# A fused attention and expert layer on one core: r by Strassen's scheme, and a reciprocal made of an exponential

## The chip, the cores and the metric

The kernel runs on one core of one Trainium2 chip. TensorE (PE) multiplies matrices, VectorE (DVE) works elementwise, ScalarE (ACT) evaluates functions, GpSimd (POOL) sets up constants and issues gathers and scatters, SyncE (SP) issues most other DMAs. Each works through its own queue in order, and they wait for one another at semaphores. The metric is the time of the whole program in device microseconds; a lower time is better.

## The reference

x is one sequence of 2048 tokens of 512 channels. xn is the layer norm of x. The result is x plus two parts.

The first is an RWKV attention: r, v, k = xn W, and, channel by channel along the tokens,

```
no = max(o, u + k);  A = exp(o - no);  Bc = exp(u + k - no)
y  = (A p + Bc v) / (A q + Bc)
o, p, q are carried on, with the decay w = -exp(time_decay)
out1 = (sigmoid(r) * y) W_out
```

The second is a mixture of experts. A softmax over 12 experts picks two per token; eight of them are small networks (silu(g) * u, 256 wide), four pass xn through, and the two chosen outputs are added with their weights.

## The kernel before, in words

**Tiling.** Channels lie on the 128 partitions in four column groups c = 0..3, tokens in four blocks b = 0..3 of 512. A unit (b, c) is one 128 x 512 piece of the recurrence. The 16 units go in the order (0,0), (1,0), (0,1), (1,1) ..., (1,3), (2,0), (3,0) ..., (3,3). The tokens of the experts are gathered into 25 tiles of 128.

**Products.** k and v of a pair of blocks are made by Strassen's scheme in Winograd's form: seven products p1 to p7 in place of eight per column group, each of two matmul steps (`two`), on sums of weights (`sum_weights`) and sums of blocks (`sum_x`). Their partial sums are taken out of PSUM in the middle, by copies on ACT (p1, p2) and additions on DVE (p3 to p7). r is made plainly: `r(b, c, h)` does two of four matmul steps, and after the fourth ACT takes exp(-r) out of PSUM into the tile that `kvr_tile` names. A matmul step in float32 shows as two instructions in the profile.

**The recurrence.** `scan(b, c)` is a generator in five stages. (1) DVE: a scan for the running maximum (L477), then a2 and b2 (L479, L480). (2) ACT: Exp of both (L482, L483). (3) DVE: the scans of the two sums (L490, L492), with b2 v between (L491). (4) DVE: den = b2 cf + sq (L497), den = (er + 1) den (L498), num = bv cf + sp (L500). (5) ACT copies the state on (L503, L504), DVE takes the reciprocal of den (L505) and multiplies num with it into yT (L506). So sigmoid(r) is part of the one division.

**Experts.** Tile i: a gather by POOL (xg), a reshaping copy on ACT (xp, L775), a transposing DMA (xq), a copy on ACT (xgT, L783), eight matmul instructions (pg, L795), tanh on ACT (th, L803), two operations on DVE (th L804, act L806), a copy on ACT (ap, L820), a transposing DMA (aq), a copy on ACT (actT, L827), four matmul instructions (po, L836), a scaled copy on ACT (yo, L840) and a scatter that adds into the output (POOL). `first_half(i)` holds pg and act of tile i, the ap of tile i-1 and the actT of tile i-2, `second_half(i)` the xgT of tile i+1, the xp of tile i+2 and the po of tile i-2.

**Order.** The schedule is manual: every engine executes in the order in which the Python code emits. From the experts on, a table sets that order. `plan(at, what)` enters one piece at a time in the table's own units; the pieces are sorted by it and emitted. Products and the output rows of blocks 0 and 1 (`attention_row`) lie one behind the other, the stages of unit u at (u-1) * unit + 4, 8, 10, 13 and 16, the halves of tile i at spread * i and spread * (i + 0.6). `unit` and `spread` follow from the number of product steps left (`left`). Behind the table come block 2's output rows, with the last stages of unit (3,3) between them, and then block 3's.

**Buffers.** PSUM pools of two banks each: ps_mm (px and r), ps_tr (py, pz), ps_gu (pg and transposes), ps_o (po and pw). The `base` pool holds the rows of xn that `attention_row` needs (three buffers); SP's queue loads them.

Of the kernel before, what the change touches and what calls it, by code (L numbers as in the profile page):

```python
# [35 lines left out]
P = 128  # L36
# [11 lines left out]
SCALE = 1.5  # L48
EPS = 1e-5
LOW = -3.0e38  # L50
O_INIT = -1.0e38
TILES = 25
MAX_TILES = 40
# [6 lines left out]
def layer(ctx: ExitStack, tc: tile.TileContext, x, w_rvk, w_out, decay, first, cls, ebias, gu, down, out):  # L60
    nc = tc.nc

    def pool(name, bufs, **kw):
        return ctx.enter_context(tc.tile_pool(name=name, bufs=bufs, **kw))
# [5 lines left out]
    gathered = pool("gathered", 2)  # L70
    wk1 = pool("wk1", 1)
    rows = pool("rows", 3)
    basep = pool("base", 3)
    rp = pool("route", 1)
    small = pool("small", 2)
    kvrp = pool("kvr", 1)
# [64 lines left out]
    make_identity(nc, ident)  # L141
    eps_sb = const.tile([P, 2], F32, tag="eps", name="eps_sb")
    nc.gpsimd.memset(eps_sb[:, 0:1], EPS)

    quarters = const.tile([P, ET], F32, tag="quarters", name="quarters")
    nc.gpsimd.tensor_add(quarters, ident[:, 0:ET], ident[:, QW : QW + ET])
# [130 lines left out]
    def kvr_tile(name, b, c):  # L277

        last = slots[name]
        n = last.index(min(last))  # L280
        last[n] = units.index((b, c))
        kvr[b, c, name] = kvrp.tile([P, TB], F32, tag=f"{name}{n}", name=f"{name}{b}_{c}")
        return kvr[b, c, name]
# [56 lines left out]
    def p1(b, c):  # L340
        ps = bank(ps_mm, "mm", f"px{b}_{c}")
        yield from two(ps, a11, xnT[b][:, 0:2], c, True)
        nc.scalar.copy(kvr_tile("v", b, c), ps)
        yield

    def p2(b, c):
        ps = banks[f"px{b}_{c}"]
        yield from two(ps, a12, xnT[b][:, 2:4], c, False)
        nc.scalar.copy(kvr_tile("k", b, c), ps)
        ready.add(("k", b, c))  # L350
        yield
# [3 lines left out]
    def p6(b, c):  # L355
        ps = bank(ps_tr, "tr", f"py{b}_{c}")
        yield from two(ps, s2, ts[b, 0][:, 1], c, True)
        out_ = kvr_tile("k", b + 1, c)
        if (b, c) < (0, 2):
            deferred.append((out_, kvr[b, c, "v"], ps))  # L360
        else:
            nc.vector.tensor_add(out_, kvr[b, c, "v"], ps)
        yield

    def p7(b, c):
        ps = banks[f"py{b}_{c}"]
        yield from two(ps, s3, ts[b, 1][:, 0], c, False)
        nc.vector.tensor_add(kvr_tile("v", b + 1, c), kvr[b, c, "v"], ps)
        yield
# [11 lines left out]
    def p4(b, c):  # L381
        ps = banks[f"py{b}_{c}"]
        yield from two(ps, a22, ts[b, 1][:, 1], c, False)
        v = kvr[b, c, "v"]
        nc.vector.tensor_add(v, v, ps)
        ready.add(("v", b, c))
        yield
# [11 lines left out]
    def r(b, c, h):  # L399

        if h == 0:
            if (b, c) == (0, 0):
                bank(ps_gu, "gu", f"pr{b}_{c}")
            else:
                bank(ps_mm, "mm", f"pr{b}_{c}")
        ps = banks[f"pr{b}_{c}"]
        for k in (2 * h, 2 * h + 1):
            nc.tensor.matmul(  # L408
                ps, wrvk_sb[0][:, k, c * P : (c + 1) * P], xnT[b][:, k, :], start=(k == 0), stop=(k == CC - 1)
            )  # L410
            if k == CC - 1:
                nc.scalar.activation(kvr_tile("r", b, c), ps, AF.Exp, scale=-1.0)
            yield

    def all_products():

        rest = iter([r(b, 3, h) for b in (0, 1) for h in (0, 1)])
        for part, c in ((p1, 0), (p1, 1), (p2, 0), (p2, 1), (p1, 2), (p1, 3), (r, 0), (p2, 2), (r, 1), (p2, 3)):
            yield from r(0, 0, c) if part is r else part(0, c)
        for c in range(3):  # L420
            for b in (0, 1):
                if (b, c) == (1, 2):
                    yield from p6(0, 0)
                    yield from p6(0, 1)
                if (b, c) != (0, 0):
                    yield from r(b, c, 0)
                    yield from r(b, c, 1)
        for part, c in (
            (p7, 0), (p7, 1), (p4, 0), (p5, 0), (p4, 1), (p3, 0),
            (p5, 1), (p6, 2), (r, 0), (p3, 1), (p6, 3), (r, 0), (p7, 2), (p7, 3),  # L430
            (p4, 2), (p4, 3), (r, 1), (p5, 2), (r, 1), (p5, 3), (p3, 2),
        ):
            yield from next(rest) if part is r else part(0, c)
        yield from p1(2, 0)
        yield from r(2, 0, 0)
        yield from p3(0, 3)
        for c in range(CC):
            if c:
                yield from p1(2, c)
                yield from r(2, c, 0)  # L440
            yield from p6(2, c)
            yield from r(2, c, 1)
            yield from p2(2, c)
            yield from p7(2, c)
            yield from r(3, c, 0)
            yield from p5(2, c)
            yield from p4(2, c)
            yield from r(3, c, 1)
            yield from p3(2, c)

    products = all_products()

# [7 lines left out]
    def scan(b, c):  # L460

        n = f"{b}_{c}"
        s = state[c]
        w, cf = wdec[:, c : c + 1], cfac[:, c : c + 1]
        assert ("k", b, c) in ready
        k = kvr[b, c, "k"]
        if c == 0:

            yT[b] = place.tile([P, NJ, CC, P], F32, tag=("s8", "s9", "s2", "s3")[b], name=f"yT{b}")


        obv = wk1.tile([P, 3, TB + 1], F32, tag="obv", name=f"obv{n}")
        nc.vector.tensor_copy(obv[:, :, 0:1], s[:, 0:3].unsqueeze(2))
        o, bs, bvs = (obv[:, m, 0:TB] for m in range(3))
        o2, b2, bv = (obv[:, m, 1 : TB + 1] for m in range(3))

        nc.vector.tensor_tensor_scan(o2, w.to_broadcast([P, TB]), k, s[:, 0:1], ALU.add, ALU.max)  # L477
        a2 = wk.tile([P, TB], F32, tag="a2", name=f"a2{n}")
        nc.vector.scalar_tensor_tensor(a2, o, w, o2, ALU.add, ALU.subtract)  # L479
        nc.vector.tensor_sub(b2, k, o2)  # L480
        yield
        nc.scalar.activation(a2, a2, AF.Exp)  # L482
        nc.scalar.activation(b2, b2, AF.Exp)  # L483
        yield

        assert ("v", b, c) in ready
        v = kvr[b, c, "v"]
        sums = wk1.tile([P, 2, TB], F32, tag="sums", name=f"sums{n}")
        sq, sp = sums[:, 0, :], sums[:, 1, :]
        nc.vector.tensor_tensor_scan(sq, bs, a2, s[:, 3:4], ALU.add, ALU.mult)  # L490
        nc.vector.tensor_mul(bv, b2, v)  # L491
        nc.vector.tensor_tensor_scan(sp, bvs, a2, s[:, 4:5], ALU.add, ALU.mult)  # L492
        yield

        er = kvr[b, c, "r"]
        den = wk1.tile([P, TB], F32, tag="den", name=f"den{n}")
        nc.vector.scalar_tensor_tensor(den, b2, cf, sq, ALU.mult, ALU.add)  # L497
        nc.vector.scalar_tensor_tensor(den, er, 1.0, den, ALU.add, ALU.mult)  # L498
        num = wk.tile([P, TB], F32, tag="a2", name=f"num{n}")
        nc.vector.scalar_tensor_tensor(num, bv, cf, sp, ALU.mult, ALU.add)  # L500
        yield
        if b + 1 < NTB:
            nc.scalar.copy(s[:, 0:3].unsqueeze(2), obv[:, :, TB : TB + 1])  # L503
            nc.scalar.copy(s[:, 3:5].unsqueeze(2), sums[:, :, TB - 1 : TB])  # L504
        nc.vector.reciprocal(den, den)  # L505
        nc.vector.tensor_mul(  # L506
            yT[b][:, :, c, :], num.rearrange("p (j t) -> p j t", j=NJ), den.rearrange("p (j t) -> p j t", j=NJ)
        )
        yield

# [449 lines left out]

    ONE = 0.86
    ROWS = [(b, j) for b in (0, 1) for j in range(NJ)]
    left = [products] * (16 * 11 - done[0])
    late = []

    def add_row(n):
# [2 lines left out]
    def attention_row(b, j):  # L969
        i = b * NJ + j  # L970
        po = ps_o.tile([P, C], F32, tag="o", name=f"pw{i}")
        for c in range(CC):
            nc.tensor.matmul(  # L973
                po, yT[b][:, j, c, :], wout_sb[:, c, :], start=(c == 0), stop=(c == CC - 1)
            )
            if c < CC - 1:
                yield
        xn = xrows[i]
        if b == 1:

            xrows[i] = yT[b][:, j].rearrange("p c t -> p (c t)")
            late.append(i)
        nc.vector.scalar_tensor_tensor(xrows[i], xn, zw[:, i : i + 1], po, ALU.mult, ALU.add)
        if b == 0 and j % 2:
            add_row(i - 1)
            add_row(i)
        yield
# [6 lines left out]
        table.append((at, iter([(what, *args)]) if args else what))  # L994

    plan(0.5, stages[0])
    plan(3, stages[0])
    for u in range(1, len(units)):

        for at in (4, 8, 10, 13, 16)[: 2 if u == len(units) - 1 else 5]:  # L1000
            plan((u - 1) * unit + at, stages[u])

    begin = 7 * unit + 1
# [18 lines left out]
    for _, work in sorted(table, key=lambda entry: entry[0]):  # L1022
        todo = next(work, None)
        if todo:
            todo[0](*todo[1:])
    for j, stops in enumerate((1, 2, 0, 0)):
        whole(attention(NTB - 2, [j]))
        for _ in range(stops):
            next(stages[-1])
# [73 lines left out]
```

## Time and profile before

| | |
|---|---|
| median of 3 runs | 379.38 us (378.77 to 379.68) |
| the profiled execution's own time | 379.29 us |
| its span | 377.5 us |
| PE busy | 358.2 us (95%) |
| DVE busy | 308.9 us (82%) |
| ACT busy | 161.5 us (43%) |
| reciprocals (L505), 16 | 53.5 us, 3345 ns each |
| matmuls of r (L408), 128 | 60.6 us busy |
| granted clock of PE | 1.0 |

The span is the profiled execution from first to last instruction; the rest of its time lies around it. A line of the groups gives line, engine, operation, output and inputs with shapes, count, then busy time in all and the mean of one in ns, then the idle time of the engine before it and what ended it. A line of the waits reads: engine, tile and line that waited, what it waited for, microseconds in all, times, the longest. In the timeline a line is start, duration, engine, line, operation, and in brackets the idle time before it with what ended it. Matmuls overlap, so a mean of 593 ns per instruction stands for one every 0.43 us.

### The profile page before, as it was taken

How to read it: one execution, taken by the hardware profiler on the slowest of the kernel's cores; microseconds unless marked ns; L12 is line 12 of the kernel's file. 1: busy time of each engine (PE TensorE's matmuls, PEld its weight loads, DVE VectorE, ACT ScalarE, POOL GpSimd, SP SyncE). 2: the span in 40 equal slices, each digit the busy share in tenths (PEclk: the TensorE clock that was granted, in tenths of full speed). 3: DMA queues.
4: the chain of work that ended last, by engine and by line, in shares of the span. 5: the costliest groups of instructions: out<-in, count | busy, mean ns of one | idle time of the engine just before them, and what ended most of it. 6: DMA issues, size and time to landing. Idle time of an engine off the chain costs nothing.

```text
span 377.5 us, 3504 instructions
## 1 busy us (share of the span) xinstructions
PE 358.2 (95%) x970; PEld 164.9 (44%) x970; DVE 308.9 (82%) x450; ACT 161.5 (43%) x274; POOL 91.4 (24%) x118
## 2 busy tenths in 40 slices
PE   0899998999999999999999999999999999999995
PEld 0565444543444444444444444444444444444343
DVE  4879899989997997987987779597769786959951
ACT  1677311232653554554556453636354555423000
POOL 5000300210203233322232224133144321102450
PEclk9999999999999999999999999999999999999999
DMA  7998944643657898889898998999999999767497
GB/s 268 399 356 322 334 141 162 227 91 132 177 126 220 257 264 250 251 230 260 220 262 237 272 265 222 271 233 319 258 280 277 290 264 248 195 188 166 93 191 191
DMA packets 63029, 88.80 MB, mean 235 GB/s; under 512 B 42208, under 2 KB 42592, under 8 KB 59232
## 3 DMA queue, kind: packets, MB, share of 16 engines
q1 hardware_dynamic: 55472, 67.85, 61.5%
q0 software_dynamic: 7536, 20.71, 23.5%
q8 instruction: 8, 0.13, 0.1%
q14 instruction: 13, 0.11, 0.1%
HBM read 63.78 MB, written 19.40 MB: 220 GB/s over the span
## 4 chain that ended last, share of the span: by engine, by line
PE 73%; DVE 17%; DMA 5%; ACT 2%; issue 2%; SPq 0%; DVEq 0%
PE pg L795 22%; PE po L836 10%; PE pr L408 9%; PE py L325 9%; PE pw L973 7%; PE pz L325 6%; PE px L325 4%; PE pw L921 4%; DMA x<-in_x_dram 3%; DVE den L505 3%; DMA wrvk<-in_w_rvk_dram 2%; DVE tok L687 2%; DVE sums L490 1%; DVE obv L477 1%; DVE st L212 1%
## 5 line engine op out<-in xcount | busy, mean ns | idle before, releaser
L795 PE MATMUL pg<-gw,xgT 128*128 128x512 f32 x200 | 90.2, 593 | 1.5 <-ACT xgT L783 1.5
L841 POOL DMA_INDIRECT out_dram<-yo,to_i x25 | 45.7, 1826 | 165.0 <-ACT yo L840 114.5
L408 PE MATMUL pr<-xnT,wrvk 128*128 128x512 f32 x128 | 60.6, 593 | 0.0
L795 PEld LDWEIGHTS pg<-gw,xgT 128*128 128x128 f32 x200 | 37.8, 190 | 49.3 <-issue 45.7
L505 DVE RECIPROCAL den<-den 128x512 f32<-128x512 f32 x16 | 53.5, 3345 | 0.0
L836 PE MATMUL po<-dw,actT 128*128 128x512 f32 x100 | 46.9, 593 | 0.5 <-ACT actT L814 0.5
L803 ACT ACTIVATE th<-pg 128x256 f32<-128x256 f32 x25 | 9.6, 384 | 85.0 <-PE pg L795 85.0
L733 POOL DMA_INDIRECT xg<-xs,token_i x25 | 27.0, 1080 | 61.9 <-ACT xp L775 28.3
L408 PEld LDWEIGHTS pr<-xnT,wrvk 128*128 128x128 f32 x128 | 24.1, 190 | 29.2 <-issue 29.2
L804 DVE SCALAR_TENSOR_TENSOR th<-th,pg 128x256 f32<-128x256 f32 x25 | 10.5, 419 | 32.1 <-ACT th L803 32.0
L325 PE MATMUL px<-xnT,wrvk 128*128 128x512 f32 x64 | 32.3, 604 | 0.0
L325 PE MATMUL py<-t,wrvk 128*128 128x512 f32 x64 | 30.7, 594 | 0.0
L783 ACT COPY xgT<-xq 128x1024 uint16<-128x1024 uint16 x25 | 28.9, 1156 | 3.9 <-DMA xq<-xp 3.8
L921 PE MATMUL pw<-wout_sb,yT 128*128 128x512 f32 (+1 forms) x72 | 28.2, 548 | 2.0 <-DVE xrows L934 1.5
L973 PE MATMUL pw<-wout_sb,yT 128*128 128x512 f32 x64 | 30.1, 592 | 0.0
L836 PEld LDWEIGHTS po<-dw,actT 128*128 128x128 f32 x100 | 18.9, 190 | 24.2 <-issue 22.7
L775 ACT COPY xp<-xg 128x1024 uint16<-128x1024 uint16 x25 | 26.1, 1044 | 5.6 <-DMA xq<-xp 4.5
L840 ACT ACTIVATE yo<-po,wplace 128x512 f32<-128x512 f32 x25 | 17.2, 686 | 23.2 <-PE po L836 23.0
L490 DVE TENSOR_TENSOR_SCAN sums<-obv,state,a 128x512 f32<-128x512 f32 x16 | 20.5, 1282 | 4.1 <-ACT obv L483 4.0
L492 DVE TENSOR_TENSOR_SCAN sums<-obv,state,a 128x512 f32<-128x512 f32 x16 | 20.5, 1284 | 0.6
L921 PEld LDWEIGHTS pw<-wout_sb,yT 128*128 128x128 f32 x72 | 13.5, 190 | 17.0 <-issue 13.4
L477 DVE TENSOR_TENSOR_SCAN obv<-wdec,state,k 128x512 f32<-128x512 f32 x16 | 20.5, 1280 | 0.0
(171 smaller groups left out, 459.0 us busy)
## 6 DMA issues: line engine op xcount, KB each, us to landing
gw<-in_gu_dram SPq DMA_DIRECT2D x25, 1024.0 KB, 5.5
dw<-in_down_dram SPq DMA_DIRECT2D x25, 512.0 KB, 5.9
x<-in_x_dram SPq DMA_DIRECT2D x16, 256.0 KB, 5.3
xs<-x SPq DMA_DIRECT2D x16, 256.0 KB, 4.9
wrvk<-in_w_rvk_dram SPq DMA_DIRECT2D x3, 1024.0 KB, 7.2
xrow<-xs SPq DMA_DIRECT2D x8, 256.0 KB, 7.0
xrows<-xs SPq DMA_DIRECT2D x8, 256.0 KB, 5.2
wout_sb<-in_w_out_dram SPq DMA_DIRECT2D x1, 1024.0 KB, 10.6
```

The costliest lines, as they stand in the source:

```text
L325: nc.tensor.matmul(ps, a[:, k, c * P : (c + 1) * P], x[:, k], start=(start and k == 0), stop=(k == 1), skip_group_check=True,)
L408: nc.tensor.matmul(ps, wrvk_sb[0][:, k, c * P : (c + 1) * P], xnT[b][:, k, :], start=(k == 0), stop=(k == CC - 1))
L477: nc.vector.tensor_tensor_scan(o2, w.to_broadcast([P, TB]), k, s[:, 0:1], ALU.add, ALU.max)
L505: nc.vector.reciprocal(den, den)
L733: nc.gpsimd.indirect_dma_start(out=xg, out_offset=None, in_=xs, in_offset=bass.IndirectOffsetOnAxis(ap=token[:, i : i + 1], axis=0),)
L775: nc.scalar.copy(xp, st[i]["xg"].bitcast(U16).rearrange("p (c h) -> p h c", h=2))
L783: nc.scalar.copy(xgT.bitcast(U16).rearrange("p c (t h) -> p c t h", h=2), st[i]["xq"].rearrange("p (h c) t -> p c t h", h=2),)
L795: nc.tensor.matmul(pg, st[i]["xgT"][:, c, :], st[i]["w"][:, c, :], start=(c == 0), stop=(c == CC - 1))
L836: nc.tensor.matmul(po, st[i]["actT"][:, c, :], st[i]["d"][:, c, :], start=(c == 0), stop=(c == IC - 1))
L841: nc.gpsimd.indirect_dma_start(out=out, out_offset=bass.IndirectOffsetOnAxis(ap=to[:, i : i + 1], axis=0), in_=yo, in_offset=None, compute ...
L921: nc.tensor.matmul(po[:, hs], yT[b][:, j, c, :], wout_sb[:, c, hs], start=(c == 0), stop=(c == CC - 1),)
L973: nc.tensor.matmul(po, yT[b][:, j, c, :], wout_sb[:, c, :], start=(c == 0), stop=(c == CC - 1))
```

## The change

Four things change in the text.

- r is taken out as tanh(r/2) instead of exp(-r), by the same one ACT operation. sigmoid(r) is then (tanh(r/2) + 1) / 2: num is multiplied by (tanh + 1), and the half goes into the reciprocal's factors.
- r of blocks 2 and 3 is made by Strassen's scheme too. Here the two halves of the weights are two neighbouring column groups, so there are seven products q1 to q7 for c = 0, 1 and seven for c = 2, 3. Sums of weights are made in place by `sum_weights_r` (four DVE operations of 128 x 256), the block sums are those that v and k use. q1 is copied out by ACT, q2 by a Tanh on ACT, the other five by DVE additions, and three finished tiles get their Tanh in place (`r_done`). A new order of p and q products stands in `all_products`.
- The reciprocal of den becomes: z = exp(-ln2/2^23 * bits(den) + seed) on ACT, with den's bits read as an integer; f = -2 den z on DVE (in den's place); (f + 1)^2 by Square on ACT; (f + 2) z, its product with num, and the product with ((f + 1)^2 + 1) on DVE. z and the square lie in the buffer of the two sums. The scan has six stages instead of five, planned at 4, 8, 10, 13, 14.5 and 16.5.
- The `base` pool has two buffers instead of three, and block 0's output rows are written in place into yT, as block 1's were.

The diff, cut to its core:

```diff
-    basep = pool("base", 3)
+    basep = pool("base", 2)
...
+    seed = const.tile([P, 2], F32, tag="seed", name="seed")
+    nc.gpsimd.memset(seed[:, 0:1], LN2 * (127.0 - 0.043 - 1.0))
+    nc.gpsimd.memset(seed[:, 1:2], 1.0)
...
-                nc.scalar.activation(kvr_tile("r", b, c), ps, AF.Exp, scale=-1.0)
+                nc.scalar.activation(kvr_tile("r", b, c), ps, AF.Tanh, scale=0.5)
...
+    def sum_weights_r(c):
+        one, two_ = slice(c * P, (c + 1) * P), slice((c + 1) * P, (c + 2) * P)
+        s1_ = sr[:, :, c // 2 * P : (c // 2 + 1) * P]
+        nc.vector.tensor_add(s1_, wr[:, 0:2, two_], wr[:, 2:4, two_])
+        nc.vector.tensor_sub(wr[:, 0:2, two_], wr[:, 0:2, one], wr[:, 0:2, two_])
+        nc.vector.tensor_sub(wr[:, 0:2, one], s1_, wr[:, 0:2, one])
+        nc.vector.tensor_sub(wr[:, 2:4, one], wr[:, 2:4, one], wr[:, 0:2, one])
+
+    def r_done(b, c):
+        t = kvr[b, c, "r"]
+        nc.scalar.activation(t, t, AF.Tanh, scale=0.5)
...
+    def q(n, b, c):
...
+        yield from two(ps, a, z, col, first_)
+        if n == 1:
+            nc.scalar.copy(kvr_tile("r", b, c + 1), ps)
+        elif n == 2:
+            nc.scalar.activation(kvr_tile("r", b, c), ps, AF.Tanh, scale=0.5)
+            sum_weights_r(c)
+        elif n == 6:
+            nc.vector.tensor_add(kvr_tile("r", b + 1, c), kvr[b, c + 1, "r"], ps)
+        elif n == 7:
+            nc.vector.tensor_add(kvr_tile("r", b + 1, c + 1), kvr[b, c + 1, "r"], ps)
+        else:
+            d, e = {4: (b, c + 1), 5: (b + 1, c + 1), 3: (b + 1, c)}[n]
+            nc.vector.tensor_add(t, t, ps)
+            r_done(d, e)
...
+            order_ = (
+                (p6, q, 2, p2, p7, q, 6, p5, p4, q, 7, p3),
+                (p1, q, 4, p6, p2, q, 5, p7, q, 3, p5, q, -1, p4, q, -2, p3),
+                (p1, q, 6, p6, p2, p7, q, 7, p5, p4, q, 5, p3, q, 3),
+                (p1, p6, p2, p7, p4, q, -4, p5, p3),
+            )[c]
...
-        nc.vector.scalar_tensor_tensor(den, er, 1.0, den, ALU.add, ALU.mult)
         num = wk.tile([P, TB], F32, tag="a2", name=f"num{n}")
         nc.vector.scalar_tensor_tensor(num, bv, cf, sp, ALU.mult, ALU.add)
+        nc.vector.scalar_tensor_tensor(num, kvr[b, c, "r"], 1.0, num, ALU.add, ALU.mult)
         yield
...
-        nc.vector.reciprocal(den, den)
-        nc.vector.tensor_mul(
-            yT[b][:, :, c, :], num.rearrange("p (j t) -> p j t", j=NJ), den.rearrange("p (j t) -> p j t", j=NJ)
+        z, sqr = sq, sp
+        nc.scalar.activation(z, den.bitcast(I32), AF.Exp, bias=seed[:, 0:1], scale=-LN2 / 2**23)
+        nc.vector.scalar_tensor_tensor(den, den, -2.0, z, ALU.mult, ALU.mult)
+        yield
+        nc.scalar.activation(sqr, den, AF.Square, bias=seed[:, 1:2])
+        nc.vector.scalar_tensor_tensor(den, den, 2.0, z, ALU.add, ALU.mult)
+        nc.vector.tensor_mul(num, num, den)
+        nc.vector.scalar_tensor_tensor(
+            yT[b][:, :, c, :], sqr.rearrange(j4, j=NJ), 1.0, num.rearrange(j4, j=NJ), ALU.add, ALU.mult
         )
...
-    left = [products] * (16 * 11 - done[0])
+    left = [products] * (16 * 11 - 4 - done[0])
...
-    plan(3, stages[0])
+    plan(2, stages[0])
+    plan(3.5, stages[0])
...
-        for at in (4, 8, 10, 13, 16)[: 2 if u == len(units) - 1 else 5]:
+        for at in (4, 8, 10, 13, 14.5, 16.5)[: 2 if u == len(units) - 1 else 6]:
...
-    for j, stops in enumerate((1, 2, 0, 0)):
+    for j, stops in enumerate((1, 3, 0, 0)):
```

## The prediction

> **What bounds the kernel now.** I read the page first (busy shares, the chain that ended last), then the waits of TensorE (PE), the busy time by stage, and last the timeline of one expert tile.
>
> ```profile
> PE 358.2 (95%) x970; PEld 164.9 (44%) x970; DVE 308.9 (82%) x450; ACT 161.5 (43%) x274; POOL 91.4 (24%) x118
> PE 73%; DVE 17%; DMA 5%; ACT 2%; issue 2%; SPq 0%; DVEq 0%
> ```
> The chain is mostly PE.
>
> ```profile
> PE pg L795 <- ACT xgT L783: 1.5, 1, 1.5
> PE pw L921 <- DVE xrows L934: 1.5, 1, 1.5
> ```
> The waits of PE: from 66 us on, hardly any. The first is at 95 us, where ScalarE (ACT) made xgT1 late because an Exp ahead of it in its queue waited for VectorE (DVE). The second is in the tail.
>
> ```profile
> 95.00:215.00 120.00, 119.85 (x279) 53.02 (x280) 103.97 (x127) 62.26 (x107) 32.26 (x22) 1.00 0.87 231
> 215.00:332.00 117.00, 117.00 (x275) 51.87 (x275) 92.86 (x116) 57.67 (x93) 35.52 (x25) 1.00 1.03 263
> 332.00:378.00 46.00, 39.61 (x100) 18.27 (x98) 31.11 (x37) 5.79 (x12) 11.89 (x11) 1.00 0.71 158
> ```
> Busy time by stage (PE, weight loads, DVE, ACT, POOL, clock, DMA): from 95 to 332 us PE has no gap at all. A microsecond of matmul less there is a microsecond less, and a new wait of PE there is a microsecond more. In the tail DVE's chain decides.
>
> The timeline of one tile (number 6; its pg begins at S = 145.47), first DVE, then ACT:
>
> ```profile
> 149.35 0.42 DVE L804 SCALAR_TENSOR_TENSOR th<-th,pg 128x256 f32<-128x256 f32 x1 [2.27 <-ACT th L803]
> 149.81 0.42 DVE L806 TENSOR_TENSOR act<-th,pg 128x256 f32<-128x256 f32 x1
> 150.15 1.28 DVE L490 TENSOR_TENSOR_SCAN sums<-obv,state,a 128x512 f32<-128x512 f32 x1
> 151.34 0.67 DVE L491 TENSOR_TENSOR obv<-obv,v 128x512 f32<-128x512 f32 x1
> 152.04 1.28 DVE L492 TENSOR_TENSOR_SCAN sums<-obv,state,a 128x512 f32<-128x512 f32 x1
> 153.25 0.73 DVE L497 SCALAR_TENSOR_TENSOR den<-obv,cfac,sums 128x512 f32<-128x512 f32 x1
> 155.28 3.35 DVE L505 RECIPROCAL den<-den 128x512 f32<-128x512 f32 x1
> ```
> ```profile
> 148.94 0.38 ACT L803 ACTIVATE th<-pg 128x256 f32<-128x256 f32 x1 [0.74 <-PE pg L795]
> 151.14 1.17 ACT L783 COPY xgT<-xq 128x1024 uint16<-128x1024 uint16 x1
> ```
> Every tile PE's pg releases ACT's th at S+3.47, and that releases DVE's th at S+3.88. All that stands behind th in DVE's queue is later: here den ends at S+8.5. ACT makes the next tile's xgT at S+5.7 to 6.8, long before PE needs it (S+10.3), because nothing ahead of it in ACT's queue waits for that late part of DVE.
>
> **The change, part by part.** Prices:
>
> ```profile
> L505 DVE RECIPROCAL den<-den 128x512 f32<-128x512 f32 x16 | 53.5, 3345 | 0.0
> L506 DVE TENSOR_TENSOR yT<-num,den 128x512 f32<-128x512 f32 x16 | 11.1, 692 | 0.5
> L840 ACT ACTIVATE yo<-po,wplace 128x512 f32<-128x512 f32 x25 | 17.2, 686 | 23.2 <-PE po L836 23.0
> ```
>
> PE. The r products of blocks 2 and 3 go from 32 to 28 (7 of 8 per pair of column groups). One product is two matmuls of 0.429 us (8 of pg take 3.43): 4 x 0.858 = 3.43 us less.
>
> DVE. Per unit, 3.35 + 0.69 (yT) + 0.70 (er) go and five operations of 0.70 come: -1.24, 16 times -19.8 us. To the r products come ten additions out of PSUM (0.68 each, 6.8) and eight of 128x256 for the weight sums, which the trace lacks. Bounds are the 256-element copy (0.29) and the 512-element add (0.69); I take 0.42, the row with the same count (L806), together 3.4. DVE loses 9.6 us, but it does not bound the middle.
>
> ACT. Per unit an Exp and a Square come, both with a column as bias. Bounds 0.60 (L412, no column) and 0.81 (L234, two); one column is L840's 0.69, which I take: +22 us, and two copies more. ACT would be half busy; its load is not the matter, its order is. [...]
>
> POOL and SP. Two memsets go before the first work. The base pool falls from three buffers to two: each of the eight xrow loads in SP's queue now waits for the addition two rows back (218.3, 233.2, 251.1 ...: some 15 us apart). It is issued about when the row before it is added, so that wait has passed 15 us earlier: nothing, and without that cover a wait in SP's queue would hold gw and the transposes behind it. POOL's row additions still wait for the same DVE instruction.
>
> The unit's chain is now DVE den, ACT Exp, DVE, ACT Square, DVE three times. Three things follow.
>
> Start: in unit (0,0), den at 83.92 leads by the steps below to a yT that ends at 89.6 instead of 90.04, and a k addition (0.6) that stood behind yT goes into the gap at Square. The next scan starts 1.0 earlier, and so xgT1: PE's idle 1.54 shrinks to 0.5. Gain 1.0.
>
> Tail: for each of the last two units the chain from den to yT was 0.78+0.61+0.66+3.38+0.69 = 6.1; it is now den 0.67, num 0.77, num 0.61, 0.72, Square with two hand-overs 0.80, 0.73, 0.73, 0.69 = 5.7. In the first of them an addition of v comes in ahead of den (+0.6) and one of k leaves the queue behind yT for the gap at Square (-0.6). Gain 2 x 0.42 = 0.85.
>
> Middle: ACT's queue now holds Exp, Square or a tanh of r that wait for DVE, and in this program's order some stand ahead of an xgT, th or actT that PE needs. I walked the built queues from tile to tile with the steps of the timeline (start to start: th 0.46, act 0.34, scan 1.2, mul 0.70, add 0.60, dependent operation 0.76, hand-over 0.05, ACT's next start 0.10 before the end). S is the start of each tile's own pg, tiles are 10.3 apart. PE stops at:
>
> 1. Tile 2 (pg2): pg1 94.05; DVE's first refining step is behind th1 and act1, ends 100.8; Square 101.55, tanh r 102.0, xgT2 103.1. PE is there at 94.05+3.54+5x0.858 = 101.9: 1.25.
> 2. Tile 5 (po3): between act4 and den of unit (1,1) stand sum_x's four operations (4.7), the sums (3.1) and two additions (1.2), so den ends 14.4 after tile 4's start, at S+4.05; Exp, a copy, Square (behind num, num, step: 6.8), ap4, th5, actT3 8.17. PE at S+6.0: 2.2.
> 3. Tile 6 (pg7): behind th6 and act6 stand the sums and the four weight additions; den ends S+10.15, Exp 10.9, xgT7 11.95. PE at 3.43+7x0.858 = 9.44: 2.55.
> 4. Tile 9 (pg10): the addition of r(2,1) ends S+8.0; its tanh, two Exps, xgT10 10.8. PE at 10.3: 0.5.
> 5. Tile 15 (pg16): sums, k addition, den 9.1, Exp 9.84, xgT16 10.9. PE at 9.44: 1.5.
> 6. Tile 19 (q3 and pg20): r(3,3)'s addition ends 8.7, its tanh, Square, xgT20 11.0. PE at 10.3: 0.75.
> 7. Tile 20 (po18): r(3,2)'s addition ends S+5.0; its tanh, ap19, th20, actT18 7.05. PE at 6.0: 0.95.
> 8. Tile 22 (p4 of column 3): it directly follows p7, in whose bank it goes on, so it waits for v(3,3)'s addition, which stands behind num and ends S+11.7. PE at 9.44: 2.3.
>
> Sum 12.0. At the other tiles the same walk leaves margins, the smallest 0.5 (pg9). Bounds: at the lower prices (0.60 on ACT, 0.29 for a weight addition) 0.1 goes at each and 0.5 more at the third, together some 1.2; at the upper (0.81, 0.69) some 2 come. What the walk leaves out bounds it from below: nothing at all, if each of these instructions finds its wait over.
>
> The sum goes against the profiled execution, 379.29 (span 377.5 and 1.79 around it; the median of the three runs is 379.38): 379.29 - 3.43 - 1.0 - 0.85 + 12.0 = 386.0.
>
> [...]
>
> **Rivals.**
> - The stalls hardly occur (faster). For it: PE's 3.43 is certain, DVE is freed of 9.6, PE waited only once for ACT before. Against it: an in-order ACT wait is just what that one wait was. With no stall 374.0; it decides below 5.3 us of stalls. Forecast for it 374 to 378.5.
> - Half of the stalls, because my walk puts DVE too late at th: 6 us, 380.0. Against it: th at S+3.88 is a measured step, and DVE waits for it in 15 of 25 tiles.
> - More than my eight: DMA is at 1.03 of its engines from 215 us, and ACT's xgT already waited twice for a transpose (3.8 us). Late xp and ap copies then cost tiles more: 390 to 394.
> [...]
>
> **How the numbers follow.** About 0.2% (0.8 us) is what a measurement can tell here from no change. Likeliest, stalls of 9 to 15: 0.60, own range 383 to 389. Half the stalls (378.6 to 383): 0.16, of which 0.05 within 0.2%. Few (374 to 378.5): 0.17. More (above 389): 0.07. The range 376.5 to 389.5 leaves out the 0.06 above it and 0.08 at the fast end.
>
> **What would show it.** PE's waits should name ACT xgT at about four places and ACT actT at two, 2 to 2.6 us the longest, and DVE v once for py near the end; ACT's waits for DVE should grow by an Exp, a Square and r. Matmuls of r should take 3.4 us less and the middle be longer all the same. DVE's busy time should fall by some 10 us, with new idle time in front of the second refining step. I am wrong if PE's waits from 95 us to the last pg sum to under 5 us.

## The result, and the profile after

The changed kernel takes 393.17 us (median of four executions, 390.28 to 396.92) where the kernel before takes 379.07. The ratio is 1.0347, 95% interval 1.0266 to 1.0428 (the comparison leaves disturbed executions out). It is slower, by about 13 us; I had forecast 386.0 with a range up to 389.5. The direction and the places were right, the size was not.

The profiled execution took 390.28, with a span of 388.5. First its page: the engines' busy times, then the slices of PE and DVE.

```profile
span 388.5 us, 3554 instructions
...
PE 360.0 (93%) x962; PEld 163.3 (42%) x962; DVE 297.6 (77%) x500; ACT 183.8 (47%) x308; POOL 91.3 (23%) x120
...
PE   0999998999899979799999999899999997998995
...
DVE  5779999899886896786878787768677767568861
```

PE has eight matmuls fewer (962 against 970), DVE has 11.3 us less to do and ACT 22.3 more. And yet the span is 11.0 longer: PE, which was at 9 in every slice of the middle, now has holes. The view of waits says for whom. Its columns: the waiting instruction, the one waited for, us in total, times, the longest.

```profile
PE pg L862 <- ACT xgT L850: 6.7, 6, 2.8
PE po L903 <- ACT actT L894: 2.9, 2, 2.2
PE py L329 <- DVE v L372: 2.3, 1, 2.3
PE po L903 <- ACT actT L881: 1.5, 1, 1.5
```

Neither xgT nor actT has anything to do with the change. ACT's own waits show why they are late: three of the instructions that the change put into ACT's queue wait for DVE there, and what is queued behind them waits too.

```profile
ACT sums L566 <- DVE den L555: 23.3, 12, 5.5
...
ACT r L435 <- DVE r L468: 14.5, 5, 3.6
ACT sums L569 <- DVE den L567: 9.8, 8, 2.0
```

These 47.6 us are mostly idle time that cost nothing; what costs is where one of them holds up an xgT or an actT that TensorE is already waiting for. The timeline at tile 6 (start, duration, engine, line, operation; in brackets the idle time before it and who ended it):

```profile
153.15 1.28 DVE L550 TENSOR_TENSOR_SCAN sums<-obv,state,a 128x512 f32<-128x512 f32 x1
...
154.14 1.88 PE L329 MATMUL py<-t,wrvk 128*128 128x512 f32 x4
...
155.78 0.42 DVE L431 TENSOR_TENSOR wrvk<-wrvk 128x256 f32<-128x256 f32 x1
156.12 0.75 DVE L555 SCALAR_TENSOR_TENSOR den<-obv,cfac,sums 128x512 f32<-128x512 f32 x1
...
156.96 0.72 ACT L566 ACTIVATE sums<-den,seed 128x512 f32<-128x512 int32 x1 [2.29 <-DVE den L555]
...
157.59 1.15 ACT L850 COPY xgT<-xq 128x1024 uint16<-128x1024 uint16 x1
...
158.79 1.55 PE L862 MATMUL pg<-gw,xgT 128*128 128x512 f32 x3 [2.77 <-ACT xgT L850]
```

DVE does the four additions of r weights (L428 to L431, 154.35 to 156.1), then den; ACT's Exp (L566) waits 2.29 us for den; xgT stands behind the Exp; PE has had nothing to do for 2.77 us when pg7 starts. From start to start (154.14 to 158.79, less four matmuls of 0.429) the stop costs 2.93, and the eight matmuls behind it take 0.11 more than 3.43.

The second thing that the profile shows I had not forecast. Behind the stop at p4 of column 3 eight matmuls of pg23 take 5.21 us instead of 3.60, and nothing waits for anything:

```profile
327.67 1.25 PE L329 MATMUL py<-t,wrvk 128*128 128x512 f32 x2 [2.28 <-DVE v L372]
...
328.72 5.21 PE L862 MATMUL pg<-gw,xgT 128*128 128x512 f32 x8
...
333.76 1.02 PE L329 MATMUL py<-t,wrvk 128*128 128x512 f32 x2
```

The windows around it tell why. After the busy times of the engines the row ends with the granted clock, the DMA share and GB/s: 1.00 before, 0.72 over six us, 1.00 again.

```profile
318.00:328.00 10.00, 7.72 (x19) 3.27 (x18) 8.05 (x12) 6.49 (x10) 1.99 (x2) 1.00 0.91 254
328.00:334.00 6.00, 6.00 (x11) 2.49 (x10) 0.22 (x1) 0.04 (x1) 0.00 (x0) 0.72 0.64 163
334.00:340.00 6.00, 6.00 (x15) 2.66 (x14) 5.18 (x9) 3.27 (x5) 0.60 (x1) 1.00 0.25 58
```

The drop costs 1.6 us in these eight matmuls. The mean clock of the execution is 0.996. Of the other three one has 0.996 too and takes 391.52; those with 0.991 and 0.987 take 394.83 and 396.92.

### The profile page after: what moved, and what is told of

Read it like the earlier page. It is cut to its first block, busy times and chain, and to the rows that moved or that the text cites. A ratio compares the mean times of both kernels' runs of the same rounds, so it can differ in the third digit from the quotient of the medians.

```text
span 388.5 us, 3554 instructions
## 1 busy us (share of the span) xinstructions
PE 360.0 (93%) x962; PEld 163.3 (42%) x962; DVE 297.6 (77%) x500; ACT 183.8 (47%) x308; POOL 91.3 (23%) x120
## 5 line engine op out<-in xcount | busy, mean ns | idle before, releaser
L862 PE MATMUL pg<-gw,xgT 128*128 128x512 f32 x200 | 92.5, 605 | 6.7 <-ACT xgT L850 6.7
L412 PE MATMUL pr<-xnT,wrvk 128*128 128x512 f32 x64 | 29.4, 594 | 0.0
L570 DVE SCALAR_TENSOR_TENSOR den<-den,sums 128x512 f32<-128x512 f32 x16 | 11.1, 692 | 16.8 <-ACT sums L569 16.0
L566 ACT ACTIVATE sums<-den,seed 128x512 f32<-128x512 int32 x16 | 11.6, 722 | 23.4 <-DVE den L555 23.3
```

The lines of the kernel that those rows point to most:

```text
L412: nc.tensor.matmul(ps, wrvk_sb[0][:, k, c * P : (c + 1) * P], xnT[b][:, k, :], start=(k == 0), stop=(k == CC - 1))
L862: nc.tensor.matmul(pg, st[i]["xgT"][:, c, :], st[i]["w"][:, c, :], start=(c == 0), stop=(c == CC - 1))
```

## The experiments

Theory A is that of the prediction: waits for DVE, put into ACT's in-order queue ahead of xgT, actT or th (and a wait of PE for DVE at p4), stop PE; to it I now add that the clock can fall behind such a stop (0.72 over 328 to 334 us above). Rival B: ACT and DVE simply have too much to do, and the stops only show where. Rivals C1 and C2: one of the two parts alone does it, the reciprocal or Strassen's r. Each kernel is compared with runs of the kernel before on the same chip; all times are medians, and all kernels do the whole computation.

**The changed kernel again (after_again).** No edit.

> The changed kernel once more, as the base for the others. Both theories: its time lies again between 390 and 397. If the TensorE clock gate has a part in it, the mean granted clock (0.996, 0.991, 0.987 in earlier executions) should account for the differences between executions: 0.001 of clock on a span of 390 is 0.4 us.

Measured: 393.21 (392.86 to 398.57), ratio 1.0387 (1.0275 to 1.0499). By their mean clock the eight executions of this kernel are: 390.3 and 391.5 at 0.996; 393.3 and 394.8 at 0.991; 392.9, 393.1 and 396.9 at 0.987; 398.6 at 0.983. The steps of the clock are those of whole drops: 3.41 us at half the clock, as from 328.54 to 331.96 us in the first profile, cost 1.7 of 390, or 0.004 of the mean clock. But the clock does not account for all differences, as I had expected it to: three executions at 0.987 differ by 4 us, and two of them are shorter than both at 0.991. Something else varies too (the kernel before, at 0.998 to 1.000, takes 378.3 to 383.1 on one chip), and the record does not show what. The profiled execution (0.987) has the same waits to 0.1 us and three drops, behind the stops of 2.23, 2.76 and 2.28 us; they cost 1.6 to 1.7 each. Its windows:

```profile
141.00:148.00 7.00, 6.15 (x11) 2.65 (x12) 6.21 (x11) 5.72 (x9) 2.21 (x2) 0.76 0.57 152
160.00:166.00 6.00, 5.69 (x10) 2.54 (x11) 3.06 (x5) 3.22 (x7) 3.06 (x2) 0.72 0.60 104
330.00:337.00 7.00, 6.49 (x11) 2.79 (x12) 1.05 (x2) 0.20 (x1) 0.00 (x0) 0.76 0.70 170
```

So the first profiled execution was a lucky one: the same stops, one drop instead of three. The last section has what the traces show of that.

**The new reciprocal alone (recip_only).**

```diff
-        yield from q(1, 2, 0)
+        yield from r(2, 0, 0)
...
-            for part in order_:
...
+            yield from p6(2, c)
+            yield from r(2, c, 1)
+            yield from p2(2, c)
+            yield from p7(2, c)
+            yield from r(3, c, 0)
+            yield from p5(2, c)
+            yield from p4(2, c)
+            yield from r(3, c, 1)
+            yield from p3(2, c)
...
-    left = [products] * (16 * 11 - 4 - done[0])
+    left = [products] * (16 * 11 - done[0])
```

> The reciprocal from an exponential and two steps stays, the second pair's r is computed plainly again (tanh kept), four products more: +3.4 us of TensorE. Theory A (ScalarE's and VectorE's queues hold waits ahead of what TensorE needs, put there by both parts): the gap at p4 of column 3 goes, and with it the clock drop behind it (2.6 + 1.6), the gaps at tiles 9, 19 and 20 go (0.8 + 1.0 + 1.0), those at tiles 2, 5, 6 and 15 stay at least in part (4 to 8.7 together); about 385, range 381 to 390. Rival C1 (the reciprocal makes all the stalls): 390 + 3.4 = 393 to 395. Rival C2 (Strassen's r makes them all): 377 to 379.

Measured: 380.71, ratio 1.0021 (0.9993 to 1.0050): no difference that this measurement can tell. My 385 was too high. PE's waits of ACT's xgT shrink to two short ones:

```profile
PE po L902 <- ACT actT L880: 1.5, 1, 1.5
...
PE pg L861 <- ACT xgT L849: 0.7, 2, 0.4
```

ACT's load is the same as in the changed kernel (183.1 us against 183.8), so ACT's load is not it. The Exp stands ahead of xgT at tile 6 just as before, but den now starts 7.94 us after the tile's matmuls before it, not 9.71 (the weight additions, 1.77, are not there), and PE comes 0.86 later since it has one more product in that tile. Together 2.63 of the 2.93. The tail's 1.5 is there with the reciprocal alone.

**Strassen's r alone (strassen_only).**

```diff
-        z, sqr = sq, sp
-        nc.scalar.activation(z, den.bitcast(I32), AF.Exp, bias=seed[:, 0:1], scale=-LN2 / 2**23)
...
+        nc.vector.reciprocal(den, den)
...
-        for at in (4, 8, 10, 13, 14.5, 16.5)[: 2 if u == len(units) - 1 else 6]:
+        for at in (4, 8, 10, 13, 16)[: 2 if u == len(units) - 1 else 5]:
```

> The second pair's r by Strassen's scheme with tanh stays, the reciprocal is VectorE's 3.35 us instruction again in five stages a unit as in the kernel before. TensorE keeps the 3.4 us, VectorE has about 10 us more than in the kernel before (twelve additions of r, eight of weights). Theory A: the gaps at p4 of column 3 and at tiles 9, 19 and 20 stay (5.4 us, and 1.6 of clock), those of Square go; 379.3 - 3.4 + 5.4 to 7 = 381 to 383, some us more where VectorE is later at act: 381 to 388. Rival C1 (the reciprocal makes all the stalls): 375 to 377. Rival C2 (Strassen's r makes them all): 389 or more.

Measured: 389.10, ratio 1.0187 (1.0082 to 1.0293). That is above the 381 to 388 expected, and by its number it is what rival C2 had forecast (389 or more). The stops of r are there as expected:

```profile
PE pg L856 <- ACT xgT L844: 4.1, 3, 2.1
PE py L329 <- DVE v L372: 3.1, 2, 2.3
PE pw L982 <- DVE xrows L995: 2.3, 1, 2.3
PE po L897 <- ACT actT L888: 1.7, 1, 1.7
```

py's 2.28 at p4, actT's 1.66 at tile 20 (behind a tanh of r that waits 4.63 us for DVE), xgT's 0.5 at tile 9. (The 1.54 of xgT at pg1 is that of the kernel before.) Others I had not expected, and they are not r's: an xgT of 2.08 at tile 21 that waited for its DMA transpose, and 2.3 us at the end, where DVE's 3.34 us reciprocal stands in the tail again. DVE is at 318.1 us. Behind two of the stops, 2.28 and 2.33, the clock fell. So neither C1 nor C2 holds. 0.2% and 1.9% alone make 3.5 to 3.9% together; these intervals are too wide to show by themselves that the whole is more than the sum, but the traces show it: at tiles 5, 6 and 15, where the changed kernel stops for 2.22, 2.77 and 1.53 us, neither part alone has a stop of more than 0.13. The two parts use up the same margin.

**Only p4 moved (p4_spaced).**

```diff
-                (p1, p6, p2, p7, p4, q, -4, p5, p3),
+                (p1, p6, p2, p7, p5, p4, q, -4, p3),
```

> Only the order of column 3 is changed: after p7 come p5 and then p4, so that the sum of v(3,3), which reads the bank that p4 goes on in, is done before TensorE is there. The order of ScalarE's instructions is that of the changed kernel. Theory A: the 2.3 us gap at p4 goes, 2.6 us counted from start to start; if the low clock of the eight matmuls behind it came of that gap, 1.6 us more: 2.6 to 4.2 under the changed kernel of the same batch. Rival B (VectorE's and ScalarE's load sets the time, the gap is only where it shows): the wait turns up again at the next tiles, within 1 us of the changed kernel.

Measured: 394.97 (391.06 to 396.62), ratio 1.0359 (1.0256 to 1.0463): not better, an expectation missed. The wait of py for v is gone from the list, but in the profiled execution pg22 waits for a transposed x, whose transpose was issued at 305.05 and let ACT go on only at 317.4:

```profile
317.40 1.16 ACT L850 COPY xgT<-xq 128x1024 uint16<-128x1024 uint16 x1 [4.87 <-DMA xq<-xp]
...
318.61 1.22 PE L862 MATMUL pg<-gw,xgT 128*128 128x512 f32 x1 [3.12 <-ACT xgT L850]
```

Behind that stop the clock is 0.59 over eight us, 3.0 us more. In the changed kernel the same transpose, issued at 304.97, was in time for 312.89. The windows from 305 to 317 us of the changed kernel and of this one end with the clock, the DMA share and GB/s:

```profile
305.00:317.00 12.00, 12.00 (x29) 5.32 (x28) 9.27 (x14) 7.43 (x13) 3.68 (x3) 1.00 1.05 299
```

```profile
305.00:317.00 12.00, 10.49 (x25) 4.37 (x23) 9.24 (x15) 3.77 (x9) 2.82 (x2) 1.00 1.07 170
```

The DMA engines are as busy and move little more than half. So a third kind of stop is at work, that of the prediction's rival with the transposes; whether the new order brings it or chance does, the run does not tell. Part of the gain is lost again at the end, too: the stop at the last tile is 2.43 us here, 1.54 in the changed kernel, and one behind it 1.85 instead of 0.52. By the total, p4's price stays open here; the kernel before_p4 measures it by itself.

**The last two stages later (late).**

```diff
-        for at in (4, 8, 10, 13, 14.5, 16.5)[: 2 if u == len(units) - 1 else 6]:
+        for at in (4, 8, 10, 13, 15.5, 17.5)[: 2 if u == len(units) - 1 else 6]:
```

> No work is changed: the last two stages of each scan unit are planned at 15.5 and 17.5 instead of 14.5 and 16.5, so that in several units ScalarE's th, actT or xgT come ahead of its Exp or Square, which wait for VectorE. Theory A (in-order waits placed ahead of what TensorE needs): the gaps at tiles 5, 6 and 15 (2.5, 3.0 and 1.8 us from start to start) shrink to under 0.6 each, and with two gaps over 2 us gone the clock rises by up to 0.008: 5 to 10 us under the changed kernel, 383 to 388. Rival B (the added work itself is too much for ScalarE and VectorE): the same sum of gaps at other places, within 2 us of the changed kernel's 393.

Measured: 385.77, ratio 1.0162 (1.0100 to 1.0224). No work is changed, and 7.4 us are gone. The busy times are those of the changed kernel (DVE 297.7, ACT 183.6). Gone are the stops at tiles 6 and 15; tile 5's is 0.30 instead of 2.22; a new one of 1.63 came at tile 19, where both Exp and Square are now ahead of xgT. This speaks against B: the same load, and PE's listed waits for xgT, actT and v fall from 13.4 us to 8.0.

**Square on VectorE (square_dve).**

```diff
-        nc.scalar.activation(sqr, den, AF.Square, bias=seed[:, 1:2])
+        nc.vector.scalar_tensor_tensor(sqr, den, 2.0, den, ALU.add, ALU.mult)
...
-            yT[b][:, :, c, :], sqr.rearrange(j4, j=NJ), 1.0, num.rearrange(j4, j=NJ), ALU.add, ALU.mult
+            yT[b][:, :, c, :], sqr.rearrange(j4, j=NJ), 2.0, num.rearrange(j4, j=NJ), ALU.add, ALU.mult
```

> The Square on ScalarE becomes one scalar_tensor_tensor on VectorE, f(f + 2) with 2 added in the last step instead of 1: 16 activations of 0.72 us and one wait of ScalarE for VectorE per unit go, VectorE gets 16 x 0.69 = 11 us. Theory A: the gaps whose last wait stands at a Square (tiles 2, 5 and part of 19) shrink, those at the Exp (tiles 6 and 15) and at p4 stay: 3 to 5 us of gaps less, and one drop of the clock less, 386 to 391. Rival B (load): VectorE's 11 us more make act, den and v later and the time longer, 395 or more.

Measured: 388.67, ratio 1.0244 (1.0197 to 1.0291), with DVE at 308.3 instead of 297.6. More work on DVE and less time, against B. The stops at tiles 2, 5 and 19 lose 2.8 us from start to start (4.5 to 1.7, a small new one behind tile 2 included); those at tiles 6, 15 and p4, which have no Square ahead, are unchanged at 2.77, 1.52 and 2.27.

**p4 behind p7 in the kernel before (before_p4).**

```diff
             yield from p7(2, c)
+            if c == CC - 1:
+                yield from p4(2, c)
             yield from r(3, c, 0)
             yield from p5(2, c)
-            yield from p4(2, c)
+            if c < CC - 1:
+                yield from p4(2, c)
```

> The kernel before with one change: in column 3 p4 follows p7 directly, so that TensorE waits for the sum of v(3,3) that reads the same bank; this is one gap of 1.5 to 2.6 us in a kernel that has none in the middle. If a gap costs only itself: 380 to 382 and a granted clock of 1.000. If the clock falls behind such a gap: 1.6 us more in those executions where the gap is over 2 us, and a mean clock of about 0.996 in them.

Measured: 382.86, ratio 1.0076 (1.0026 to 1.0126), with one stop made in a kernel that had none there:

```profile
PE py L325 <- DVE v L368: 2.1, 1, 2.1
```

This is p4's price by itself, 2.26 us from start to start. Its four executions split by clock: 380.83 and 382.19 at 0.999 and 1.000, 384.04 and 383.53 at 0.996 and 0.995. By their clocks, then, the stop of 2.1 us was followed by a drop in two executions of four, for 2.3 us in the mean; only the profiled execution, 380.83 without a drop, has a trace.

**Later stages and p4 moved (late_p4).** The edits of the two kernels above.

> Both orders together, later last stages and p4 behind p5 in column 3. Theory A: no gap over 1.5 us is left between 95 us and the last tile, so hardly any drop of the clock: the clock 0.996 or more and 378 to 384. Rival B: as without the p4 order, within 2 us. A third way, the DMA transposes (a transposed x that lands late at the end, as the kernel with the p4 order alone had it at tile 22, 3.1 us and 3.0 more behind it): a wait of xgT for DMA in the last tiles and 385 to 390.

Measured: 383.80, ratio 1.0109 (1.0063 to 1.0155). The stop at p4 is gone and no transpose is late, so 2 us come of it. Left are 1.62 at tile 19, 0.71 at tile 20, and one at the last tile, which has grown from 1.54, as it did when p4 alone was moved:

```profile
PE po L903 <- ACT actT L881: 2.4, 1, 2.4
```

There ACT's copy of the last tile's turned act stands behind the tanh, Exp and Square of unit (2,3); the clock drops behind it. The time is at the upper end of the 378 to 384 expected, but the clock is not (0.990 to 0.996, where 0.996 or more was expected).

**All orders (v_all, v_all_sq, recip_all).** To the above: xgT's copy planned by itself and earlier, the last act turned earlier, the last r product between p7 and p4; with Square on ACT, with Square on DVE, and with plain r.

```diff
-        if i + 1 < n:
-            unite(i + 1)
...
+        if i + 1 < TILES:
+            plan(4 + spread * (i + 0.45), unite, i + 1)
+        if i + 2 < TILES:
+            plan(4 + spread * (i + 0.6), flip, i + 2)
...
-    plan(4 + spread * TILES, turn_act, TILES - 1)
+    plan(1 + spread * TILES, turn_act, TILES - 1)
...
-                (p1, p6, p2, p7, p5, p4, q, -4, p3),
+                (p1, p6, p2, p7, q, -4, p4, p5, p3),
```

> Orders only, no work changed against the changed kernel: later last stages (15.5, 17.5); in column 3 the last r product between p7 and p4; the copy of the next tile's transposed x issued 1.5 us earlier and by itself; the last tile's transposition of act issued 3 us earlier, so that its ScalarE copy stands ahead of the Exp and Square of unit (2,3). Theory A: the gaps left with the later stages and the p4 order (1.8 and 0.9 at tiles 19 and 20, 0.7 at tile 9, 0.8 at tile 2, 2.4 and a low clock at the last tile) go for the most part, TensorE keeps the 3.4 us of four products: 375.5 to 379, at or below the kernel before. Rival B (load of ScalarE and VectorE, or DMA from 215 us on): the gaps go elsewhere, 382 to 385 as with the later stages and the p4 order.

> The same orders and the Square as f(f + 2) on VectorE (11 us more there, one wait of ScalarE per unit less). Theory A: with ScalarE's waits no longer ahead of what TensorE needs, the Square's place matters little, in the middle within 1 us of the version with ScalarE's Square; the tail gains or loses 0.3. Rival B: VectorE's 11 us show as 2 us or more.

> The new reciprocal with plain r (no Strassen for r) and the same orders but for column 3, which is as in the kernel before. If TensorE alone sets the time there, the only gains are those at the start and in the last columns: 377.5 to 379.5. It tells what Strassen's r is worth once the orders are mended: theory A expects 2 to 3.4 us more here than with it.

Measured: v_all 384.50, ratio 1.0105 (1.0072 to 1.0139); v_all_sq 381.07, ratio 1.0017 (0.9986 to 1.0048); recip_all 379.38, ratio 0.9996 (0.9956 to 1.0037). The first two expectations were missed; so was that recip_all would be slower than v_all, while its own range was met. In v_all the stops moved from xgT to actT:

```profile
PE po L903 <- ACT actT L894: 4.5, 3, 2.4
PE pw L984 <- DVE xrows L997: 2.0, 1, 2.0
```

Taken alone this looks like B. The timeline of v_all at tile 11 (the next expectation calls it tile 10) says otherwise: the tanh of r that the change put directly behind VectorE's addition waits 4.54 us, and behind it stand ap, th and actT:

```profile
200.29 0.68 DVE L538 TENSOR_TENSOR obv<-k,obv 128x512 f32<-128x512 f32 x1
...
200.89 0.68 DVE L468 TENSOR_TENSOR r<-r,qz 128x512 f32<-128x512 f32 x1
201.60 0.63 ACT L435 ACTIVATE r<-r 128x512 f32<-128x512 f32 x1 [4.54 <-DVE r L468]
...
202.92 0.66 ACT L894 COPY actT<-aq 128x512 uint16<-128x512 uint16 x1
...
203.63 1.55 PE L903 MATMUL po<-dw,actT 128*128 128x512 f32 x3 [1.84 <-ACT actT L894]
```

**The tanh of r issued later (v_defer_sq, v_defer).** To v_all_sq and v_all:

```diff
     def r_done(b, c):
-        t = kvr[b, c, "r"]
-        nc.scalar.activation(t, t, AF.Tanh, scale=0.5)
-        ready.add(("r", b, c))
+        summed.append((b, c))
+    def turn_r():
+        while summed:
+            b, c = summed.pop(0)
+            t = kvr[b, c, "r"]
+            nc.scalar.activation(t, t, AF.Tanh, scale=0.5)
+            ready.add(("r", b, c))
...
+        turn_r()
         nc.scalar.activation(a2, a2, AF.Exp)
```

> All the changed orders with Square on VectorE, and the tanh of a Strassen r is issued ahead of the next unit's Exp instead of directly behind VectorE's addition, so that ap, th and actT of tile 20 no longer stand behind it. Theory A (ScalarE's waits in its queue): the 2.2 us gap at tile 20 goes, and with it about half of the executions with a clock of 0.996; 376.5 to 379, under the kernel before's 379.5. Rival B (load, DMA): another wait in the same tiles takes its place, 380 to 382.

> The same with Square on ScalarE. Theory A: the gaps of 1.84 us at tile 10 and 2.39 us at tile 20, where a tanh or Square waits ahead of actT, shrink to under 1 us at the second; a Square of unit (0,2) may keep the first; 379 to 382. Rival B: 383 to 385 as without it.

Measured: v_defer_sq 378.65, ratio 0.9969 (0.9942 to 0.9996); v_defer 377.35, ratio 0.9933 (0.9906 to 0.9961). The first is in its range, the second below its 379 to 382. It is 2.5 us faster than the kernel before, and 16 us faster than the changed kernel, with the same arithmetic. Lines of v_defer's page, and of its view of PE's waits:

```profile
span 374.6 us, 3552 instructions
...
PE 355.5 (95%) x962; PEld 163.3 (44%) x962; DVE 297.8 (80%) x500; ACT 183.9 (49%) x308; POOL 91.0 (24%) x120
```

```profile
PE pw L994 <- DVE xrows L1007: 2.0, 1, 2.0
...
PE pg L872 <- ACT xgT L860: 1.0, 2, 0.6
...
PE po L913 <- ACT actT L904: 0.3, 1, 0.3
```

DVE and ACT have the loads of the changed kernel, and between 95 and 330 us the only listed stops are 0.60 of xgT at tile 2 and 0.29 of actT at tile 5: the load of ACT and DVE does not set the time of the middle. That refutes B there. The base pool has two buffers here too, and no stop in the middle comes of that. With these orders Strassen's r is worth about 2.0 us against recip_all (377.35 and 379.38, intervals that just touch), of 3.4 by the count of its matmuls. What is left is the last xrows, 2.0 us, where the chain over DVE of the last two units ends last.

## Why the prediction was wrong

By its steps:

- **PE, -3.43:** right in the count, eight matmuls of 0.429.
- **DVE and ACT busy time:** -9.6 and +22 forecast, -11.3 and +22.3 measured (Exp and Square 0.72 us each, where 0.69 was taken); both beside the path, as said.
- **Start, -1.0:** right. From start to start the stop before pg1 fell by 1.11 (1.81 to 0.70).
- **The eight stops, +12.0:** all eight are there, at the places and with the causes named. Idle time by place, forecast and measured: 1.25 and 1.08; 2.2 and 2.22; 2.55 and 2.77; 0.5 and 0.52; 1.5 and 1.53; 0.75 and 0.49; 0.95 and 0.72; 2.3 and 2.28. Sum 12.0 and 11.6. (By the steps written there, the third and the seventh come to 2.51 and 1.05 rather than 2.55 and 0.95.) But idle time is not what a stop costs. From start to start they cost 14.0: the column reads 0.16 short at each, since ends of matmuls are modelled, and the group behind each takes 0.10 longer. The trace of before had one such pair to read it from, pg1 with 1.54 idle and 1.81 from start to start. A ninth, small one at tile 17, where ACT's xgT waits 2.91 us for a DMA transpose, costs 0.33.
- **Tail, -0.85:** wrong in sign. From the first matmul behind pg24 to the end it is 44.2 us against 44.0. The chain did become shorter: unit (3,3) gained 0.46 from its sums to yT, and unit (2,3) 0.19 from th to the next unit's scan. What was lost, 0.83, lies between them. The last tile's po waits 1.54 us for an actT whose copy is queued behind unit (2,3)'s Square, so the output products (pw) come late, and the addition of xrows that stands ahead of unit (3,3)'s sums in DVE's queue waits 0.94 for them. The kernel with the reciprocal alone has this 1.5 too. I had reckoned the length of the chain and not who shares ACT's queue with it.
- **The clock, 0:** the missing term. I took a matmul at 0.429 throughout. A drop costs 1.7 us, all of its matmuls counted: 1.7 in the profiled execution, about 4.9 in the one with three drops, and some 4 in the mean of all eight executions, if their mean clocks are read as one to four drops. In that mean it is the largest term.

The lines of the tail, in the changed kernel:

```profile
353.05 0.72 ACT L569 ACTIVATE sums<-den,seed 128x512 f32<-128x512 f32 x1 [0.93 <-DVE den L567]
...
354.08 1.99 PE L903 MATMUL po<-dw,actT 128*128 128x512 f32 x4 [1.54 <-ACT actT L881]
...
359.54 0.75 DVE L1001 SCALAR_TENSOR_TENSOR xrows<-xrows,zw,pw 128x512 f32<-128x512 f32 x1 [0.94 <-PE pw L988]
```

For the profiled execution the sum closes: 386.0, and 1.7 (clock), 2.0 (edges of the eight), 0.3 (a ninth), 1.0 (tail); less 0.1 (start), 0.5 (PE was that much earlier at 91 us) and 0.3 (a small stop of the kernel before at 109 us that is gone) make 390.1, against 390.28. The median lies 2.9 above that execution. It is the mean of 391.52, whose clock shows one drop as well, and of 394.83, whose clock shows two; so the clock explains about 0.9 of the 2.9, and the rest stays open, since only one of the four executions has a trace.

So the mechanism stood, and the failed steps are sizes: the price of a stop, which I read from the idle column alone (12.0, measured 14.0), the tail (-0.85, measured +0.2) and the clock (0, measured 1.7 in the profiled execution, more in most others by their mean clock). Without the clock's part the profiled execution would have been 388.6, inside my range. But the eight executions less 1.7 for each drop are 387.8 to 391.8, in the mean 389.9, just above it: the clock alone does not make the miss.

Of the rivals none came. "More than eight" named the right time (390 to 394) by the wrong means: in the changed kernel's middle a late DMA transpose held up one pg, by 0.23 us (tile 17). In some of the experiments they did more (2.08 us in strassen_only, 3.12 in p4_spaced, 1.08 in recip_all). Square as a multiplication on VectorE brought 2.8 us at tiles 2, 5 and 19 (square_dve), and in v_all, where the tanh of r still stands ahead of actT, 3.4 in all (384.50 against 381.07). But between v_defer and v_defer_sq, where the orders are mended, ACT's Square is no worse (0.9933 against 0.9969, the intervals overlap): here it was the wait ahead of xgT and actT that cost, not the engine.

## What to carry to other kernels

Before giving work to an engine because it is idle half of the time, look at what stands behind the new instruction in that engine's queue and when its operand is ready; a hand-over to and fro cost here where another consumer's copy was queued behind it (2.93 us at tile 6), not where it ran. Price a stop of TensorE from start to start, and where it is some 2 us or more add the chance of a drop of the clock (here behind 12 of 23 stops of 1.98 to 3.12 us, 1.6 to 1.8 us each and once 3.0). A change that loses by waits may win after re-ordering alone: here the same arithmetic gave 393.2 and 377.4 us.

## What was unexpected in the hardware

The granted clock falls behind some short stops of TensorE and not behind others. In fourteen profiles (both kernels, and every experiment but v_all_sq) I took every stop of 1 us or more between 85 and 386 us, and the clock over the next 4 us. Of 22 stops of 1.08 to 1.84 us none was followed by a clock under 1.00. Of 23 stops of 1.98 to 3.12 us 12 were, with 0.50 to 0.68 over these 4 us, and the same stop of the same kernel goes either way (2.77 us at tile 6: 1.00 in one execution, 0.58 in the other). A drop costs 1.6 to 1.8 us, 3.0 after the longest stop (p4_spaced).

The clock in the changed kernel's first profile tells the two kinds apart. It is 1.00 or 0.50 there: it falls at 328.54 us, is back at 331.96, and falls again behind the program's end, at 389.98. These changes lie 3.41 us and 17 times 3.41 us apart. Cut that trace, behind its first 15 us, into windows along these steps: the drop begins at the end of the one window that holds 2.00 us or more of TensorE's listed idle time (2.28, the stop at p4), and no window with 1.86 or less is followed by the start of one. The two long stops without a drop lie across the edge of two windows, 2.77 as 1.86 and 0.91, 2.22 as 1.01 and 1.21. The other seven profiles with a drop agree, as far as the clock over 4 us places its start: the 3.41 us ahead of each drop hold about 2.0 us or more of listed idle time (the least, 2.0, in v_all), and steps of 3.41 us counted from it cut each of their five long stops without a drop in two, the larger part some 1.2 to 1.7. In p4_spaced the low stretch takes about 6.9 us (0.96 over 314 to 318 us, 0.59 over 318 to 326) and begins some 2.2 us into the stop of 3.12. The other four of the 11 long stops without a drop lie in profiles that have none at all, and nothing places the steps there. The two executions of tile 6 differ in the same way. The stop lies from 156.02 to 158.79 us in the changed kernel's first profile and from 157.55 to 160.31 in its second (after_again). The windows around it, with PE's busy time in front and the clock third from the end:

```profile
154.46:157.87 3.41, 1.56 (x4) 0.38 (x2) 3.20 (x7) 1.10 (x3) 0.00 (x0) 1.00 0.72 283
157.87:161.28 3.41, 2.49 (x6) 1.25 (x7) 1.35 (x3) 3.41 (x5) 0.74 (x1) 1.00 0.10 21
```

```profile
156.84:160.25 3.41, 0.71 (x2) 0.00 (x0) 3.27 (x6) 1.76 (x3) 0.00 (x0) 1.00 0.53 223
160.25:163.66 3.41, 3.35 (x4) 1.52 (x5) 1.32 (x3) 2.67 (x5) 1.59 (x1) 0.50 0.39 73
```

In the first the idle time is split into 1.86 and 0.91 us, in the second 2.70 lie in one window. The edges lie at another point of the program in each of the two, and I take this for the chance in it. If every position is equally likely, an estimate from these numbers (windows of 3.41 us, a bound of 2.0, between the 1.86 and the 2.00 seen) gives a stop of 2.0 us a drop in 41% of the executions, one of 2.3 in 50%, one of 2.8 in 65%; over the 23 stops that makes 11.5, and 12 were seen. No run moved a stop on purpose to test the bound.
